# Four state-space layers on one core: B's products shared out by turn, the projection moved, seven buffers for B and C

## The chip, the cores and the metric

One core of a Trainium2 chip runs the whole program. The time is device microseconds of one execution; 18841.26 us before, the median of three runs (18840.8 to 18842.25). A smaller number is better. The engines are named as the profile names them: PE (matmul), PEld (its weight loads), DVE (vector), ACT (scalar, activation functions), POOL (GpSimd), SP (the queue that issues every DMA here).

## The reference, cut to what matters

The input is 8 images of 48 x 48 positions and 96 channels. Four residual layers follow one another, each on a group-normed input. Layers 0 and 3 are a two-dimensional selective scan, layer 1 an up- and down-sampled pointwise network, layer 2 a one-dimensional selective scan along rows and columns. The scans take nearly all the time. In one direction k of one image, with 192 inner channels d and 16 states n:

```
delta = softplus(dt_proj(x_proj(u)) + bias)             # u = silu(conv(in_proj(x)))
h[t, d, n] = exp(delta[t, d] * A[d, n]) * h[t-1, d, n] + (delta[t, d] * u[t, d]) * B[t, n]
y[t, d]    = sum_n h[t, d, n] * C[t, n]
```

There are four directions in each of these layers. In layers 0 and 3 the sum of the directions is normed, multiplied with silu(z) and projected; in layer 2 each direction is multiplied with its own silu(z) and projected.

## The kernel before

**Blocks, slots and turns.** A direction of an image is cut into 5 blocks of 10, 10, 10, 10 and 8 rows of 48 positions (480 or 384 positions). The 192 x 16 pairs (d, n) of a block are laid out as 24 units of 128 partitions. A block has 8 slots of 3 units, and 4 turns of 2 slots. The buffers `rooms` hold a turn each, and are taken in rotation. A layer has 8 x 4 x 5 = 160 blocks.

**What a turn does.** Six units pass through these steps, and every engine works through its own instructions in the order in which the program writes them (there is no scheduler):
- `make_da` (L288, ACT): exp(A * delta) into a PSUM tile for 2 units. There are two such tiles, so a pair can be made only when the scan two pairs earlier is done.
- `copy_b` (L245, ACT): the slot's B is copied to the one PSUM tile `ps_b`, from which DVE reads it. The next copy waits until DVE has read the last one.
- `make_dbu` (L264, DVE or POOL): (delta * u) * B for the slot's 3 units, a turn ahead. The table `ON_POOL` says how many of a slot's units POOL makes; POOL reads B from SBUF and needs no copy.
- `scan` (L296, DVE): the recurrence, two units at a time, three scans a turn.
- `make_hc` (L302, POOL): h * C in place, 3 units an instruction.
- `reduce` (L318, L322, L324, PE): the sums over n by matmul into `ps_y`; four slots close a sum, which ACT (layers 0 and 3, L683) or DVE (layer 2, L834) takes away in `finish`.

The loop over turns (L375 to L404) writes them in this order: scan 0, `make_hc` of the last turn's second slot, B's products of the next turn, `make_da`, `reduce` of the last turn's first slot, scan 1, `make_da`, `copy_b`, B's products, `reduce` of the second slot, `aside`, `make_hc`, `make_da` of the next turn's first pair, scan 2, `copy_b`, `finish`, `aside`.

**What goes beside it.** `aside` runs once a slot (twice a turn). In this order it issues loads of B and C (`load_bc`, L229; slots in `LOAD_BC`) and of delta and delta * u (`load_dd`, L217; slots in `LOAD_DD`) for the next block, takes one step of the generator `side`, and then runs the steps of `stage1` that fall on the slot. `stage1` prepares a block two blocks ahead. In layers 0 and 3: `s0` (slot 0) projects u to B, C and dt's input in the PSUM tile `s1`, of which there is one; `s1` (slot 1) has ACT copy it to `bcl` (L647); `s3` stores B and C to DRAM (L650) and starts dt's matmuls (L632); slots 4 and 5 add the bias (L636); `s6` (slot 6) is the Softplus (L660); slots 7 and 8 multiply with u on POOL (`make_du`, L449); slots 9 and 10 store the result to DRAM (`store_dd`, L434), whence `load_dd` broadcasts it to 128 partitions. In layer 2 the steps lie on slots 3 to 11: two convolutions (L771), a Silu in slot 6 (L778), the projection (L788), `bcl` (L793), a Softplus in slot 8 (L806), POOL's products, a Silu of z in slot 10 (L820), and the stores in slots 10 and 11.

**The side generator of layers 0 and 3** runs through an image's 160 slots: `post` of the last image (55 slots), `front` (group norm) of the next, a filler up to slot 80, and then `conv` of the next image: ten half blocks of eight steps 0 to 7, in which the matmul of z (L517) is in step 6 and the two Silus (L521, L523) in step 7. Before the change a half block starts on slot 0 of a block.

**Functions of ACT.** Exp, Softplus, Silu and Sqrt need different tables. Each change of function puts an ACT_TABLE_LOAD in ACT's queue, and another when Exp comes back.

Of the kernel before, what the change touches and what calls it, by code (L numbers as in the profile page):

```python
# [9 lines left out]
F32 = mybir.dt.float32  # L10
# [7 lines left out]
DH = 96  # L18
# [11 lines left out]
NG = 8  # L30
ORDER = [(0, sg) for sg in range(4)] + [(1, sg) for sg in range(3, -1, -1)]
LOAD_BC = (2, 3, 6, 7)
LOAD_DD = (4, 5)
NBUF = 6
UP = 96
UG = 73
UR = 7
# [1 line left out]
NM = 3  # L39
FAR = 1e30  # L40
CH = 96
ON_POOL = {1: 2, 3: 2, 5: 3, 7: 2}


DIRS_SS = [(False, False), (True, False), (False, True), (True, True)]
# [50 lines left out]
def vss_stack_kernel(ctx: ExitStack, tc: tile.TileContext, i: dict, out: bass.AP):  # L96
# [86 lines left out]
        yield  # L183


    def scans(dirs, order, restart, a, pools, ps, stage1, opening, done, side, tail):

# [46 lines left out]
        def copy_b(t):  # L234

            if t >= NG * len(blocks):
                return
            b, slot = blocks[t // NG], t % NG
            if slot == NG // 2:
                bps[t] = bps[t - 1]  # L240
                return
            if ON_POOL.get(slot) == 3:
                return
            bps[t] = ps("b", 1)
            nc.scalar.copy(bps[t][:, :bcs[t][0].shape[1]], bcs[t][0])  # L245
# [4 lines left out]
        def make_dbu(t, engine):  # L250

            if t >= NG * len(blocks):
                return
            b, slot = blocks[t // NG], t % NG
            if t // 2 not in dbus:
                dbus[t // 2] = rooms[t // 2 % (NG // 2)]
            cut = 3 - ON_POOL.get(slot, 0)
# [6 lines left out]
            engine.tensor_mul(o, du, by.unsqueeze(1).to_broadcast([P, hi - lo, by.shape[1]]))  # L264
# [13 lines left out]
        def make_da(t, pair):  # L278
            if t >= nt:
                return  # L280
            b, q = turns[t]
            da = ps("da", 2, 1024)
            das[t, pair] = da
            for u in (2 * pair, 2 * pair + 1):
                half, sg = ORDER[2 * q + u // 3]
                ci = half * 12 + sg * 3 + u % 3
                at = (u - 2 * pair) * b.m
                nc.scalar.activation(da[:, at:at + b.m], b.got[half][:, u % 3, 0, :], AF.Exp, scale=a[:, b.k, ci:ci + 1])  # L288
# [43 lines left out]
        def plan(b, at):  # L332
            b.got = {}
            sources(b, pools)
            for n, step in stage1(b).items():
                steps.setdefault(at + n, []).append(step)
# [2 lines left out]
            for step in steps.pop(t, []):  # L339
                step()  # L340

        for n, b in enumerate(blocks[:2]):
            plan(b, NG * (n - 2))
        for t in range(-2 * NG, 0):
            run(t)
        begin(0)
        begin(1)
# [27 lines left out]
        for t, (b, q) in enumerate(turns):  # L375
            at, nblk = 2 * t, t // (NG // 2)
            if q == 0:
                if nblk + 2 < len(blocks):
                    plan(blocks[nblk + 2], at)
                if b.k == order[0] and b.first:  # L380
                    beside = side(b.job)
            scan(t, 0)
            if t > 0:
                make_hc(t - 1, 1)
            make_dbu(at + 2, nc.vector)
            make_da(t, 1)
            make_dbu(at + 3, nc.gpsimd)
            if t > 0:
                reduce(t - 1, 0)
            scan(t, 1)  # L390
            make_da(t, 2)
            copy_b(at + 3)
            make_dbu(at + 3, nc.vector)
            if t > 0:
                reduce(t - 1, 1)
            aside(at)
            begin(t + 2)
            make_hc(t, 0)
# [61 lines left out]
    def ss2d(l, xin, xout, b0=0):  # L460
# [2 lines left out]

        def pool(name, bufs, **kw):
            return stack.enter_context(tc.tile_pool(name=name, bufs=bufs, **kw))
        wt, big, zp, lnp, xio = pool("wt", 1), pool("big", 3), pool("z", 1), pool("ln", 2), pool("xio", 2)
        zdr = pool("zdr", 3, space=DRAM)
        w = weights(wt, [f"{l}_{n}" for n in ("in", "cb", "xp", "dtb", "a", "d", "nw", "nb", "out")])
        dtw = wt.tile([NBC, NK, 2, DH], F32, tag="dtw", name="dtw")
# [27 lines left out]
        def load_x(b):  # L497
            nc.sync.dma_start(xpad[:C, 1:1 + H, 1:1 + W], seq(xin[b], False))

        def conv(b, blks):  # L500
            if blks[0] == BLKS[0]:
                us[b] = big.tile([DH, 2, L], F32, tag="big", name="u")
                zs[b] = zdr.tile([DH, 2, L], F32, tag="z", name="zd")
            for r0, nr in blks:
                n = nr * SEG
                for half in range(2):
                    pu = side_psum()
                    for slot in range(7):
                        for tap in ((0,), (1, 2), (3,), (4, 5), (6,), (7, 8), ())[slot]:
                            dy, dx = tap // 3, tap % 3  # L510
                            at = (2 * tap + half) * DH
                            nc.tensor.matmul(pu[:, :n], lhsT=flat[:, at:at + P],  # L512
                                             rhs=xpad[:, r0 + dy:r0 + dy + nr, dx:dx + W],
                                             start=(tap == 0), stop=(tap == 8))
                        if slot == 6:
                            pz = ps("s1", 1)
                            nc.tensor.matmul(pz[:DH, :n], lhsT=w[f"{l}_in"][:, (2 + half) * DH:(3 + half) * DH],  # L517
                                             rhs=xpad[:C, 1 + r0:1 + r0 + nr, 1:1 + W], start=True, stop=True)
                        yield
                    s = slice(r0 * W, r0 * W + n)  # L520
                    nc.scalar.activation(us[b][:, half, s], pu[:DH, :n], AF.Silu, bias=w[f"{l}_cb"][:, half:half + 1])  # L521
                    z = zp.tile([DH, BMAX], F32, tag="z", name="z")
                    nc.scalar.activation(z[:, :n], pz[:DH, :n], AF.Silu)  # L523
                    yield
                    nc.sync.dma_start(zs[b][:, half, s], z[:, :n])

# [61 lines left out]
        def side(job):  # L588
            used = 0
            more = job + 1 < nb  # L590
            if job == 0:
                for n, _ in enumerate(conv(0, BLKS[3:])):
                    if n % 2:
                        used += 1
                        yield
            if more:
                load_x(job + 1)
            if job > 0:

                for _ in range(3):  # L600
                    used += 1
                    yield
                for _ in post(job - 1):
                    used += 1
                    yield
            if more:
                for _ in front(job + 1):
                    used += 1
                    yield
                while used < 10 * NG:  # L610
                    used += 1
# [12 lines left out]

        def stage1(b):
# [33 lines left out]
                both = b.dds[:, :, 0, b.at]  # L659
                nc.scalar.activation(both, both, AF.Softplus)  # L660

            def du(half):
                return lambda: make_du(b, half, u[:, half])

            def store(half):
                return lambda: store_dd(b, half)

            return {0: s0, 1: s1, 3: s3, 4: s4, 5: lambda: biased(1), 6: s6, 7: du(0), 8: du(1),
                    NG + 1: store(0), NG + 2: store(1)}

        def so_far(b, half):
            if b.job not in yss:
# [10 lines left out]
            nc.scalar.copy(so_far(b, half), rows(y[:DH], b.n))  # L683
            return []

        dirs = DIRS_SS
# [5 lines left out]
        scans(dirs, (0, 1, 3, 2), False, a, pools, ps, stage1, opening, done, side, [])  # L692
        for _ in post(nb - 1, BLKS[:1]):
            pass
        stack.close()
# [2 lines left out]
    def lines(xin, xout):  # L698
# [56 lines left out]
        def stage1(b):  # L755
# [112 lines left out]
        load_x(0)  # L868
        for _ in front(0):
            pass  # L870
        scans(dirs, range(NK), True, a, pools, ps, stage1, opening, done, side, tail)
        stack.close()


# [286 lines left out]
```

## Time and profile before

| | |
|---|---|
| median of three runs | 18841.26 us |
| the profiled execution: time, span | 18848.6 us, 18846.8 us |
| layer 0, first to last scan | 119.3 to 5733.4 us |
| layer 1 (no scans) | to 7166.7 us |
| layer 2, first to last scan | 7166.7 to 13077.1 us |
| layer 3, first to last scan | 13204.3 to 18816.7 us |
| busy: DVE, POOL, PE, ACT | 16139.5, 15203.6, 14864.5, 13830.0 us |

The profiled execution is 1.8 us longer than its span, and 7.3 us (0.04%) longer than the median. A busy share is an average over the whole span. Layer 1 has little for DVE and POOL, so in the scan layers their shares are higher than in that average. A row of costliest groups has the line, the engine, the operation, what it writes and reads, the count, the busy time, the mean time of one, and the idle time of the engine just before such an instruction with what ended it. In a timeline, the columns are the start and the duration in microseconds; idle time before an instruction stands in brackets.

### The profile page before, as it was taken

The page shows a single profiled execution, that of the slowest core. Times are in us where ns is not written, and L with a number is a line of the kernel's source. Part 1 is how long each engine was busy: PE and PEld are TensorE (multiplying, and loading weights), DVE is VectorE, ACT ScalarE, POOL GpSimd, SP SyncE. Part 2 cuts the span into 40 slices and gives each one's busy share as a digit, 9 for nine tenths or more (in the row PEclk, how much of TensorE's full clock was granted, in tenths as well). Part 3 has the DMA queues.
Part 4 walks back from the last instruction along what each step waited for, and adds up shares of the span by engine and source line. Part 5 has one row for each costly group of instructions (what it writes and reads, how often), then busy time and mean ns, then how long its engine had stood idle before and what let it go on. Part 6 is the DMA issues. An engine that isn't in the chain of part 4 may idle for free.

```text
span 18846.8 us, 169421 instructions
## 1 busy us (share of the span) xinstructions
PE 14864.5 (79%) x53500; PEld 4298.7 (23%) x53500; DVE 16139.5 (86%) x10809; ACT 13830.0 (73%) x20502; POOL 15203.6 (81%) x8316
## 2 busy tenths in 40 slices
PE   6777777777777897888988988888677777777776
PEld 1211211211214562222222222222121121121121
DVE  7999999999993227999999999997999999999998
ACT  6777777777772227888888888886778778778776
POOL 7899899899891007888888888886899999999998
PEclk7776776776767787888888888888777777677776
DMA  4545445445453334444444444443454554554444
GB/s 138 167 166 166 167 166 168 165 166 170 161 171 60 48 46 141 154 146 153 156 147 150 151 155 148 148 154 119 164 170 162 169 170 161 169 168 161 169 166 146
DMA packets 768461, 2836.57 MB, mean 151 GB/s; under 512 B 235724, under 2 KB 298668, under 8 KB 640926
## 3 DMA queue, kind: packets, MB, share of 16 engines
q1 hardware_dynamic: 767558, 2825.75, 45.5%
q8 instruction: 418, 6.85, 0.2%
q14 instruction: 485, 3.97, 0.1%
HBM read 2377.32 MB, written 448.17 MB: 150 GB/s over the span
## 4 chain that ended last, share of the span: by engine, by line
DVE 24%; PE 21%; ACT 18%; POOL 17%; issue 12%; DMA 7%; SPq 0%; POOLq 0%; DVEq 0%; ACTq 0%
DVE dbu L296 15%; POOL dbu L302 12%; DVE dbu L264 7%; ACT ps_da L288 5%; PE ps_s L771 4%; ACT L288 4%; POOL dbu L264 4%; DMA dd<-dd 3%; PE ps_y L322 3%; DMA dd<-dds 2%; PE ps_h L1001 2%; PE ps_y L1014 2%; POOL dds L449 1%; PE ps_side L512 1%; PE ps_s L642 1%
## 5 line engine op out<-in xcount | busy, mean ns | idle before, releaser
L296 DVE TENSOR_TENSOR_SCAN dbu<-ps_da,dbu 128x968 f32<-128x968 f32 (+3 forms) x5760 | 11853.6, 2076 | 1080.1 <-ACT ps_da L288 1002.8
L302 POOL TENSOR_TENSOR dbu<-dbu,bc 128x1440 f32<-128x1440 f32 (+1 forms) x3840 | 10060.1, 2634 | 1877.1 <-DVE dbu L296 1715.4
L288 ACT ACTIVATE ps_da<-dd,w_l_a 128x484 f32<-128x484 f32 (+3 forms) x11520 | 7440.1, 650 | 2865.8 <-DVE dbu L296 2652.9
L322 PE MATMUL ps_y<-dbu,w_red 128*32 128x480 f32 (+1 forms) x23040 | 4834.2, 736 | 2581.2 <-POOL dbu L302 2578.1
L324 PE MATMUL ps_y<-dbu,w_red 128*32 128x480 f32 (+1 forms) x7680 | 4795.5, 736 | 0.0
L264 DVE TENSOR_TENSOR dbu<-dd,ps_b 128x1443 f32<-128x1443 f32 (+7 forms) x3360 | 3895.9, 1159 | 292.9 <-ACT ps_b L245 217.5
L264 POOL TENSOR_TENSOR dbu<-dd,bc 128x962 f32<-128x962 f32 (+7 forms) x1920 | 3889.3, 2026 | 96.5 <-DMA dd<-dd 50.0
L322 PEld LDWEIGHTS ps_y<-dbu,w_red 128*32 128x32 f32 x23040 | 756.2, 125 | 6399.6 <-POOL dbu L302 4693.7
L771 PE MATMUL ps_s<-xpad,w_l_cw 128*128 128x480 f32 (+1 forms) x2560 | 1753.3, 837 | 2.6 <-ACT xpad L144 1.6
L245 ACT COPY ps_b<-bc 128x482 f32<-128x482 f32 (+3 forms) x2880 | 1543.4, 536 | 283.4 <-DVE dbu L264 257.3
L512 PE MATMUL ps_side<-xpad,w_l_cw 128*128 128x480 f32 (+1 forms) x2880 | 1613.8, 688 | 5.8 <-ACT xpad L144 4.5
L288 ACT ACT_TABLE_LOAD x986 | 1265.0, 1283 | 17.3
L133 POOL MEMSET w_l_cw<- 128x1760 f32 (+1 forms) x3 | 5.8, 1942 | 1344.4 <-DVE x L981 1339.0
L642 PE MATMUL ps_s<-u,w_l_xp 96*38 96x480 f32 (+1 forms) x1280 | 932.9, 868 | 2.8 <-ACT dds L636 1.5
L632 PE MATMUL ps_s<-bcl,dtw 6*96 6x480 f32 (+1 forms) x1280 | 830.1, 735 | 125.2 <-ACT dds L636 114.9
L449 POOL TENSOR_TENSOR dds<-dds,u 96x480 f32<-96x480 f32 (+1 forms) x640 | 765.8, 1196 | 182.9 <-ACT dds L660 182.8
L318 PE MATMUL ps_y<-ysum,w_ident 96*96 96x480 f32 (+1 forms) x960 | 754.3, 875 | 134.1 <-ACT ysum L683 133.2
L512 PEld LDWEIGHTS ps_side<-xpad,w_l_cw 128*128 128x128 f32 x2880 | 571.2, 223 | 1119.3 <-issue 922.3
L771 PEld LDWEIGHTS ps_s<-xpad,w_l_cw 128*128 128x128 f32 x2560 | 517.5, 207 | 1075.5 <-issue 976.0
L324 PEld LDWEIGHTS ps_y<-dbu,w_red 128*32 128x32 f32 x7680 | 693.7, 125 | 0.0
L788 PE MATMUL ps_s<-ub,w_l_xp 96*38 96x480 f32 (+1 forms) x640 | 376.8, 724 | 271.9 <-ACT ub L778 271.8
L812 PE MATMUL ps_s<-xpad,w_l_inz 96*96 96x480 f32 (+1 forms) x640 | 506.7, 926 | 79.7 <-ACT dds L806 60.2
(147 smaller groups left out, 11761.0 us busy)
## 6 DMA issues: line engine op xcount, KB each, us to landing
dd<-dd SPq DMA_DIRECT2D x512, 1452.0 KB
bc<-bcd SPq DMA_DIRECT2D x1536, 480.0 KB
dd<-dd SPq DMA_DIRECT2D x256, 1440.0 KB
dd<-dds SPq DMA_DIRECT2D x512, 363.0 KB
dd<-dd SPq DMA_DIRECT2D x128, 1164.0 KB
bc<-bcd SPq DMA_DIRECT2D x384, 384.0 KB
dd<-dds SPq DMA_DIRECT2D x256, 360.0 KB
dd<-dd SPq DMA_DIRECT2D x64, 1152.0 KB
```

The source lines that it names most:

```text
L245: nc.scalar.copy(bps[t][:, :bcs[t][0].shape[1]], bcs[t][0])
L264: engine.tensor_mul(o, du, by.unsqueeze(1).to_broadcast([P, hi - lo, by.shape[1]]))
L288: nc.scalar.activation(da[:, at:at + b.m], b.got[half][:, u % 3, 0, :], AF.Exp, scale=a[:, b.k, ci:ci + 1])
L296: nc.vector.tensor_tensor_scan(db, da, db, 0.0, ALU.mult, ALU.add)
L302: nc.gpsimd.tensor_mul(h, h, bcs.pop(2 * t + sub)[1].unsqueeze(1).to_broadcast([P, 3, n]))
L322: nc.tensor.matmul(y[32 * g:32 * g + 32, :n], lhsT=wc["red"][:, :32], rhs=hc[:, g, b.at], start=False, stop=(slot == 3))
L324: nc.tensor.matmul(y[DH:, :n], lhsT=wc["red"][:, 32:], rhs=hc[:, 2, b.at], start=(slot == 0), stop=(slot == 3))
L449: nc.gpsimd.tensor_mul(rows(du, n), rows(dt, n), u)
L512: nc.tensor.matmul(pu[:, :n], lhsT=flat[:, at:at + P], rhs=xpad[:, r0 + dy:r0 + dy + nr, dx:dx + W], start=(tap == 0), stop=(tap == 8))
L632: nc.tensor.matmul(got["p"][:DH, :n], lhsT=dtw[2 * NS:, b.k, half, :], rhs=b.bcl[2 * NS:, :n], start=True, stop=True)
L642: nc.tensor.matmul(got["p"][:NBC, :n], lhsT=w[f"{l}_xp"][:, b.k, half, :], rhs=u[:, half], start=(half == 0), stop=(half == 1))
L771: nc.tensor.matmul(got["u", half][:, :n], lhsT=flat[:, at:at + P], rhs=shifted(off), start=(tap == 0), stop=(tap == 3))
```

## The change

- `ON_POOL` becomes two tables. In both, and before, POOL makes 9 of a block's 24 units; what differs is the slots. Before, DVE makes 4, 3, 4 and 4 units in turns 0 to 3. In layers 0 and 3 it now makes 2, 5, 2 and 6, in layer 2 it makes 4, 3, 2 and 6. POOL may now also make units of a turn's first slot, for which the loop has another call.
- `copy_b` copies no B for slots that POOL makes alone. It is 6 copies a block in layers 0 and 3 as before, and 5 in place of 6 in layer 2.
- `plan` is called a block earlier for the same slots, so that a step can lie on slot -1. In layers 0 and 3 `s0` moves to the last slot of the block before (ahead of the sums of the last turn), both `make_du` to slot 7, and the stores to slots 8 and 9.
- `LOAD_DD` goes from slots 4 and 5 to 3 and 5, in all three layers.
- There are seven buffers for B and C in place of six. `xio` goes from two buffers to one and layer 2's `zb` from three to two.
- `conv` of the next image starts five slots sooner, on slot 3 of a block. Its Silus so fall on slot 2, in the second turn. The matmul of z is put at the end of `aside`, behind the slot's steps.

```diff
-LOAD_DD = (4, 5)
-NBUF = 6
+LOAD_DD = (3, 5)
+NBUF = 7
...
-ON_POOL = {1: 2, 3: 2, 5: 3, 7: 2}
+ON_POOL_SS = {2: 1, 3: 3, 5: 1, 6: 1, 7: 3}
+ON_POOL_L2 = {3: 2, 5: 3, 6: 1, 7: 3}
...
-            if slot == NG // 2:
+            if on_pool.get(slot) == 3:
+                return
+            if slot == NG // 2 and t - 1 in bps:
                 bps[t] = bps[t - 1]
-                return
-            if ON_POOL.get(slot) == 3:
                 return
...
-        for n, b in enumerate(blocks[:2]):
+        for n, b in enumerate(blocks[:3]):
             plan(b, NG * (n - 2))
-        for t in range(-2 * NG, 0):
+        for t in range(-2 * NG - 1, 0):
             run(t)
...
-                if nblk + 2 < len(blocks):
-                    plan(blocks[nblk + 2], at)
+                if nblk + 3 < len(blocks):
+                    plan(blocks[nblk + 3], at + NG)
...
             make_dbu(at + 2, nc.vector)
             make_da(t, 1)
+            make_dbu(at + 2, nc.gpsimd)
             make_dbu(at + 3, nc.gpsimd)
...
-        wt, big, zp, lnp, xio = pool("wt", 1), pool("big", 3), pool("z", 1), pool("ln", 2), pool("xio", 2)
+        wt, big, zp, lnp, xio = pool("wt", 1), pool("big", 3), pool("z", 1), pool("ln", 2), pool("xio", 1)
...
-        def conv(b, blks):
+        def conv(b, blks, behind=lambda step: step()):
...
                         if slot == 6:
-                            pz = ps("s1", 1)
-                            nc.tensor.matmul(pz[:DH, :n], lhsT=w[f"{l}_in"][:, (2 + half) * DH:(3 + half) * DH],
-                                             rhs=xpad[:C, 1 + r0:1 + r0 + nr, 1:1 + W], start=True, stop=True)
+                            got = {}
+
+                            def gate():
+                                got["z"] = ps("s1", 1)
+                                nc.tensor.matmul(got["z"][:DH, :n], lhsT=w[f"{l}_in"][:, (2 + half) * DH:(3 + half) * DH],
+                                                 rhs=xpad[:C, 1 + r0:1 + r0 + nr, 1:1 + W], start=True, stop=True)
+                            behind(gate)
                         yield
...
-                while used < 10 * NG:
+
+                while used < 10 * NG - 5:
                     used += 1
                     yield
-                yield from conv(job + 1, BLKS)
+                yield from conv(job + 1, BLKS, tail.append)
...
-            return {0: s0, 1: s1, 3: s3, 4: s4, 5: lambda: biased(1), 6: s6, 7: du(0), 8: du(1),
-                    NG + 1: store(0), NG + 2: store(1)}
+            return {-1: s0, 1: s1, 3: s3, 4: s4, 5: lambda: biased(1), 6: s6, 7: du,
+                    NG: store(0), NG + 1: store(1)}
...
-                b.zb = up.tile([DH, 2, BMAX], F32, tag="zb", name="zb")
+                b.zb = up.tile([DH, 2, BMAX], F32, tag="zb", name="zb", bufs=2)
```

More of the change, by code (lines that the diff above doesn't have):

```diff
@@ L183, in norm_scale, with scans @@
         yield
-    def scans(dirs, order, restart, a, pools, ps, stage1, opening, done, side, tail):
+    def scans(dirs, order, restart, on_pool, a, pools, ps, stage1, opening, done, side, tail):
         blocks = [Block(job, k, blk, n == 0, n == len(BLKS) - 1, dirs[k][1])
@@ L256, in make_dbu @@
                 dbus[t // 2] = rooms[t // 2 % (NG // 2)]
-            cut = 3 - ON_POOL.get(slot, 0)
+            cut = 3 - on_pool.get(slot, 0)
             lo, hi = (0, cut) if engine is nc.vector else (cut, 3)
@@ L522, in conv @@
                     z = zp.tile([DH, BMAX], F32, tag="z", name="z")
-                    nc.scalar.activation(z[:, :n], pz[:DH, :n], AF.Silu)
+                    nc.scalar.activation(z[:, :n], got["z"][:DH, :n], AF.Silu)
                     yield
@@ L660, in s6, with du @@
                 nc.scalar.activation(both, both, AF.Softplus)
-            def du(half):
-                return lambda: make_du(b, half, u[:, half])
+            def du():
+                for half in range(2):
+                    make_du(b, half, u[:, half])
             def store(half):
                 return lambda: store_dd(b, half)
-            return {0: s0, 1: s1, 3: s3, 4: s4, 5: lambda: biased(1), 6: s6, 7: du(0), 8: du(1),
-                    NG + 1: store(0), NG + 2: store(1)}
+            return {-1: s0, 1: s1, 3: s3, 4: s4, 5: lambda: biased(1), 6: s6, 7: du,
+                    NG: store(0), NG + 1: store(1)}
         def so_far(b, half):
@@ L684, in done @@
             return []
-        dirs = DIRS_SS
+        dirs, tail = DIRS_SS, []
         load_x(0)
@@ L691, in ss2d @@
             pass
-        scans(dirs, (0, 1, 3, 2), False, a, pools, ps, stage1, opening, done, side, [])
+        scans(dirs, (0, 1, 3, 2), False, ON_POOL_SS, a, pools, ps, stage1, opening, done, side, tail)
         for _ in post(nb - 1, BLKS[:1]):
@@ L870, in lines @@
             pass
-        scans(dirs, range(NK), True, a, pools, ps, stage1, opening, done, side, tail)
+        scans(dirs, range(NK), True, ON_POOL_L2, a, pools, ps, stage1, opening, done, side, tail)
         stack.close()
```

## The prediction

> **What bounds the kernel now.** I read the busy shares first, then DVE's waits, then the timelines of DVE and ACT over one turn.
>
> ```profile
> PE 14864.5 (79%) x53500; PEld 4298.7 (23%) x53500; DVE 16139.5 (86%) x10809; ACT 13830.0 (73%) x20502; POOL 15203.6 (81%) x8316
> ```
> ```profile
> DVE dbu L296 <- ACT ps_da L288: 1002.8, 826, 4.1
> ...
> ACT bcl L647 <- PE ps_s L642: 340.4, 136, 5.8
> ```
>
> DVE is the fullest engine, and layer 1 leaves it half idle. From 470 to 5180 us (layer 0) it is busy 93%, POOL 91%, ACT 78%, PE 76%. So a scan layer is DVE's work plus DVE's idle time, and the idle time is what can be won. Summed over the timeline between first and last scan it is 394 us in layer 0, 389 in layer 3, 529 in layer 2. Most of it is one wait: the scan stands ready, and ACT has not made its exp. The two timelines show why. First a Softplus (layer 0, end of turn 3):
>
> ```profile
> 3730.47 1.63 DVE L264 TENSOR_TENSOR dbu<-dd,ps_b 128x1443 f32<-128x1443 f32 x1
> 3732.02 2.16 DVE L296 TENSOR_TENSOR_SCAN dbu<-ps_da,dbu 128x968 f32<-128x968 f32 x1
> 3734.10 0.63 DVE L264 TENSOR_TENSOR dbu<-dd,ps_b 128x481 f32<-128x481 f32 x1
> ...
> 3737.57 2.17 DVE L296 TENSOR_TENSOR_SCAN dbu<-ps_da,dbu 128x968 f32<-128x968 f32 x1 [0.69 <-ACT ps_da L288]
> ```
> ```profile
> 3732.14 0.57 ACT L245 COPY ps_b<-bc 128x482 f32<-128x482 f32 x1 [0.18 <-DVE dbu L264]
> 3732.72 1.28 ACT L660 ACT_TABLE_LOAD   x1
> 3734.01 0.85 ACT L660 ACTIVATE dds<-dds 96x768 f32<-96x768 f32 x1
> 3734.88 1.28 ACT L288 ACT_TABLE_LOAD   x1
> 3736.17 1.37 ACT L288 ACTIVATE ps_da<-dd,w_l_a 128x484 f32<-128x484 f32 x2
> ```
>
> The exp of the next turn's first pair stands behind the Softplus and two loads: it ends 7.07 us after the turn's first product began. DVE would be there after 6.4. Then a Silu of `conv`, a slot later:
>
> ```profile
> 2011.15 1.28 ACT L521 ACT_TABLE_LOAD   x1
> 2012.44 0.66 ACT L521 ACTIVATE u<-ps_side,w_l_cb 96x480 f32<-96x480 f32 x1
> 2013.00 0.56 ACT L523 ACTIVATE z<-ps_s 96x480 f32<-96x480 f32 x1
> 2013.58 1.28 ACT L288 ACT_TABLE_LOAD   x1
> ```
> ```profile
> 2016.27 2.17 DVE L296 TENSOR_TENSOR_SCAN dbu<-ps_da,dbu 128x968 f32<-128x968 f32 x1 [1.87 <-ACT ps_da L288]
> ```
>
> By turn, layer 0's idle time is: 113 us ahead of the first scan of turn 0 (Softplus), 134 ahead of its second (Silu, some 70 blocks at 1.87), 53 ahead of turn 1's second scan, 38 put down to POOL, the rest small waits for PE. Layer 3 repeats this. The 53 belong to the second wait above: ACT's copy to `bcl` stands for PE's projection, which PE runs only after sums that wait for POOL. Layer 2 has 238 ahead of turn 0 (Silu of slot 6), 112 ahead of turn 1 (Softplus), 20 ahead of turn 2, 63 at its adds (L849, L851), 59 for `dd` loads, 37 others.
>
> **What the Trainium skill says.** "ScalarE: Activation LUTs", section "What ACT_TABLE_LOAD costs", gives 1283 ns for a load and some 1380 ns of drain. The trace agrees on the load; it shows the next instruction 0.02 us later, so I use 1.28. "Perfetto Trace Analysis", section "Identifying Performance Opportunities", says that a repeated bubble can mean that too few buffers are there; here it is the order of ACT's queue. "GPSIMD Engine Reference", section "Specifications", says that POOL shares its SBUF interface with DVE and contends when DVE has two SBUF inputs. DVE's scans and products read one of theirs from PSUM, and POOL's `make_hc` stays at 2.73 to 2.75 us; so I keep POOL's durations when DVE becomes denser.
>
> **The change, step by step** (10-row blocks; starts of successive DVE instructions: scan 2.09, product of three units 1.55, of one 0.54, of two by halving the difference 1.05).
>
> 1. *Units by turn, layers 0 and 3.* DVE's 15 units a block stay: four products of three and three of one (7.8 us) become three of three and three of two (7.8). Work: no gain. Turn 3 gets longer: from its first product, 1.55 + 2.09 + 1.55 + 2.09 = 7.3 us to the next turn, against ACT's 7.1 to 7.3 (8-row or 10-row Softplus). The Softplus wait goes, but for 8-row blocks (two in ten at about 1 us). 113 becomes 25: **88 us**.
> 2. *Silus in the second turn.* The 134 go. In turn 1 DVE takes 1.55 + 2.09 + 1.05 + 2.09 = 6.8 us after its first scan; ACT takes a copy that ends at 2.2, the Silus 3.8, the exp 1.37: 7.4. New wait 0.6 us in 70 blocks, more in the short ones: 45. **90 us**. z's matmul now stands on PE behind `bcl`'s copy, which ends about 8.5 us into the block; the Silus need it at 11.
> 3. *Projection a slot sooner.* It (2 to 2.8 us on PE) runs before the sums of turn 3, and `bcl` finds it done: **50 of the 53 us**. The price: those sums end later, perhaps 6.7 us into the block; ACT asks at 7.2. Its cover is this half microsecond, plus 2 us until a late ACT stops DVE.
> 4. *POOL.* Per block 8 `make_hc` at 2.69, 21.5; units: three of one and two of three. A product of one unit has no row; by the step from 1.89 (two) to 2.74 (three) it is 1.04, at least 0.9, so 8.6 against 8.4; `make_du` 2.0 to 2.5 and 0.3 of memsets. 32.4 to 32.9, against DVE's 32.9 plus side work. Turns 0 and 2 hold 9.2 us of POOL against 7.3 of DVE, turns 1 and 3 give it back; POOL runs up to 2.5 us late. Its units for turn 1 end at 8.3 us, DVE wants them at 10.9. I take 0.25 us of new waits a block, from 0 to 1: **minus 80** over 320 blocks. PE's sums and side matmuls come later with POOL: **minus 20** a layer.
> 5. *Stores and loads, layers 0 and 3.* On SP both `dd` stores go out a slot sooner, `dd`'s first load too; the store of z moves from slot 0 to 3, between that load and B's and C's store. SP will wait there for the Silus until about 14 us into the block; the loads behind it are needed after 25. One `xio` buffer makes 64 loads of x wait on SP for the store before them, a few us each. All hidden by loads that land several us early: 0.
> 6. *Layer 2.* Its turn 0 is as before, so the Softplus's 112 stay. Turn 3 gains a us of DVE work from turn 2, against the 1.5 us mean wait behind the Silu of slot 6. But the Silu also needs a convolution (7.7 us on PE). Where rows are convolved (half of the blocks) PE is done 6 us earlier: 1.0 us won, 80 us. Where columns are, it ends just as ACT comes (the second half's Silu waits up to 0.8 us), and the wait only changes its name: 0.2 us, 16. **96 us**, from 0 to 180. One copy of B fewer (0.55 us of ACT) lies beside other work. `dd`'s first load now goes out ahead of the second store. The first store took 10.2 us to land with the other beside it and should take less; its 59 us of waits are held by the shorter turns before it: 0, from -60 to 50. The second load and B's and C's behind it come 1 to 2 us later, with about 2 us to spare. `zb` with two buffers: DVE's last read is a turn before ACT's write: 0.
>
> Sum: 2 x (88 + 90 + 50 - 20) - 80 + 96 = 432 us. From the profiled execution's 18848.6 that gives 18417; less the 7 us by which it lies over the median, **18410**.
>
> **The rivals.**
> - *POOL becomes the bound* in layers 0 and 3. For: 91% busy already, and 32.9 us a block is DVE's own work. Against: POOL waits for DVE's scans for 391 us in 4600. Blocks would take some 34.5 us in place of 35.1 (both lengths mixed). 320 x 0.6 = 190 and half of layer 2: 18600. Chance 0.15.
> - *Everything hides*: no new wait after the Silus or from POOL, layer 2 wins 180, and the small PE waits go too. 432 + 80 + 90 + 40 + 84 = 726: 18115. Chance 0.08.
> - *The sums come too late* (slower). Projection and side matmuls now stand ahead of turn 3's sums on PE, and POOL's `make_hc` ahead of these is later. ACT takes the finished sum in its own order; if it is done later than 9 us into the block, each further us goes to the exp of turn 1 and so to DVE. It decides against the change from 11.3 us on. At 12.5 us the cost is 3 us in 320 blocks less the sum above: 18840 + 960 - 430 = 19370. For: `bcl` waited as much as 5.8 us for PE. Against: PE has 24% free here. Chance 0.06.
> - *Layer 2's chain and the exchange of waits return all*: within 0.2% of before. Chance 0.03.
>
> **The numbers.** Forecast 0.68, the others as given. Within 0.2%, about 38 us, a measurement of this kernel cannot tell a change from none. Faster: 0.68 + 0.15 + 0.08 = 0.91. Same 0.03, slower 0.06. The range 18150 to 18730 holds the forecast's own bounds (the unknowns of 4, 2 and 6 together make some 200 us either way) and most of the first two rivals.
>
> **What would show it.** Right: DVE's waits for ACT's exp (L288) fall from 1003 us to under 500; no wait ahead of turn 0's second scan; about 0.6 us ahead of turn 2's first scan in blocks with Silus; `bcl`'s 340 us gone; POOL above 93% in layers 0 and 3; layer 2's wait ahead of turn 0 shorter in row blocks alone. Wrong: DVE waiting for POOL's products, ACT waiting for `ps_y`, or a layer 0 longer than 5500 us.

## The result, and the profile after

The changed kernel takes **18727.88 us** (median of four runs, 18719.84 to 18741.66); the kernel before takes 18841.75 us beside it. The ratio is 0.994, 95% interval 0.9922 to 0.9957: 114 us faster, where 432 were forecast. The profiled execution has a span of 18720.7 us, 126 less than before. The scan layers, from first to last scan in the timelines of the two kernels, show where that comes from:

| us | before | after | change | forecast |
|---|---|---|---|---|
| layer 0 | 5614.1 | 5481.3 | -133 | -168 |
| layer 2 | 5910.4 | 6055.0 | **+145** | -96 |
| layer 3 | 5612.4 | 5483.1 | -129 | -168 |

(The forecast's 168 are 88 + 90 + 50 - 20 and half of the 80 for POOL.) Three quarters of the gain in layers 0 and 3 came. Layer 2 turned against the change.

The busy shares of the profile after:

```profile
PE 14799.0 (79%) x53500; PEld 4319.5 (23%) x53500; DVE 16219.3 (87%) x10329; ACT 13661.6 (73%) x20342; POOL 15238.6 (81%) x8639
```

DVE has fewer instructions than before and 80 us more work. In a stretch of layer 0, from 500 to 5000 us, it is now busy for 4330 us (96%; before 4180), POOL for 4206 (93%; before 4083).

DVE's waits after the change (engine and line, what it waited for, us in total, times, longest):

```profile
DVE dbu L298 <- ACT ps_da L290: 511.7, 579, 3.4
...
DVE dbu L266 <- ACT ps_b L247: 353.1, 94, 88.4
```

The second of these rows was there before, but with six waits only:

```profile
DVE dbu L264 <- ACT ps_b L245: 217.5, 6, 88.0
```

and this is the row of ACT's waits, after the change, to which it leads:

```profile
ACT ps_b L247 <- DMA bc<-bcd: 345.4, 141, 12.4
```

The wait for the exp has halved (1002.8 before), and `bcl`'s 340.4 us for the projection are down to 6.2. In their place stands a chain that the scan layers did not have before: DVE's product waits for ACT's copy of B, and the copy waits for the DMA that brings B. Between the first and the last scan of layer 2 these are 136 us of DVE and 322 us of ACT. The 217 us of before, which are still there, all lie outside the scan layers as the table counts them, at their starts.

The steps aimed at layers 0 and 3 can be seen in one stretch of layer 0. DVE after, then ACT after, in columns of start, duration, instruction and idle time in brackets:

```profile
2059.07 1.64 DVE L266 TENSOR_TENSOR dbu<-dd,ps_b 128x1443 f32<-128x1443 f32 x1
2060.61 4.26 DVE L298 TENSOR_TENSOR_SCAN dbu<-ps_da,dbu 128x968 f32<-128x968 f32 x2
...
2079.42 2.17 DVE L298 TENSOR_TENSOR_SCAN dbu<-ps_da,dbu 128x968 f32<-128x968 f32 x1 [0.53 <-ACT ps_da L290]
```
```profile
2057.68 1.28 ACT L668 ACT_TABLE_LOAD   x1
2058.98 1.00 ACT L668 ACTIVATE dds<-dds 96x960 f32<-96x960 f32 x1
2060.00 1.28 ACT L290 ACT_TABLE_LOAD   x1
2061.30 1.37 ACT L290 ACTIVATE ps_da<-dd,w_l_a 128x484 f32<-128x484 f32 x2
```

The Softplus at 2057.68 stands beside a turn with two products of three units; the exp is done at 2062.67, just as turn 0's first scan follows turn 3's last without a gap (the pair of scans from 2060.61). The Silus, in turn 1 (ACT from 2074.30, the exp behind them done at 2079.39), cost turn 2's first scan 0.53 us here, where the prediction had 0.6.

Layer 2 is another picture. SP issues the stores of `dd` (delta and delta * u), its loads and the loads of B and C in one queue. The timeline of SP before, one block of layer 2 (issue time, time in issue):

```profile
9025.08 0.73 SPq L434 DMA_DIRECT2D dd<-dds  x1
9025.85 0.54 SPq L229 DMA_DIRECT2D bc<-bcd  x1
9026.83 1.21 SPq L434 DMA_DIRECT2D dd<-dds  x1
9035.37 6.36 SPq L217 DMA_DIRECT2D dd<-dd  x2
9042.26 3.21 SPq L229 DMA_DIRECT2D bc<-bcd  x2
```

and after:

```profile
9008.11 0.74 SPq L437 DMA_DIRECT2D dd<-dds  x1
9008.90 0.54 SPq L231 DMA_DIRECT2D bc<-bcd  x1
9019.06 0.51 SPq L219 DMA_DIRECT2D dd<-dd  x1
9019.67 0.73 SPq L437 DMA_DIRECT2D dd<-dds  x1
9031.00 0.53 SPq L219 DMA_DIRECT2D dd<-dd  x1
9031.58 1.24 SPq L231 DMA_DIRECT2D bc<-bcd  x2
```

Before, both stores (360 KB each) were in flight together: the first landed 10.2 us after its issue, the second 14.3, and the B and C of the last row were issued 17.2 us after the first store. After, `dd`'s first load stands between the stores, and SP waits at it until the first store has landed (10.9 us). Only then does the second go out (11.2 us). The B and C of the last row are issued 23.5 us after the first store, 6.3 us later than before. ACT and DVE pay for it in the timelines of the same block after:

```profile
9038.50 0.56 ACT L247 COPY ps_b<-bc 128x480 f32<-128x480 f32 x1 [4.71 <-DMA bc<-bcd]
```
```profile
9039.10 1.66 DVE L266 TENSOR_TENSOR dbu<-dd,ps_b 128x1440 f32<-128x1440 f32 x1 [3.12 <-ACT ps_b L247]
```

### The profile page after: what moved, and what is told of

The parts are those of the page before. It is cut to its first block, busy times and chain, and to the rows that moved or that the text cites. A ratio compares the mean times of both kernels' runs of the same rounds, so it can differ in the third digit from the quotient of the medians.

```text
span 18720.7 us, 168607 instructions
## 1 busy us (share of the span) xinstructions
PE 14799.0 (79%) x53500; PEld 4319.5 (23%) x53500; DVE 16219.3 (87%) x10329; ACT 13661.6 (73%) x20342; POOL 15238.6 (81%) x8639
## 4 chain that ended last, share of the span: by engine, by line
POOL 29%; DVE 16%; DMA 16%; PE 15%; issue 14%; ACT 9%; SPq 1%; POOLq 0%; DVEq 0%; ACTq 0%
POOL dbu L304 20%; DVE dbu L298 10%; DMA dd<-dds 8%; POOL dbu L266 6%; DMA bc<-bcd 6%; DVE dbu L266 4%; ACT ps_da L290 4%; PE ps_y L324 2%; POOL dds L452 2%; PE ps_h L1010 2%; PE ps_s L780 2%; PE ps_y L1023 2%; ACT L290 1%; PE ps_side L515 1%; PE ps_a L1000 1%
## 5 line engine op out<-in xcount | busy, mean ns | idle before, releaser
L266 DVE TENSOR_TENSOR dbu<-dd,ps_b 128x962 f32<-128x962 f32 (+5 forms) x2880 | 3831.1, 1330 | 387.8 <-ACT ps_b L247 353.1
L266 POOL TENSOR_TENSOR dbu<-dd,bc 128x481 f32<-128x481 f32 (+5 forms) x2240 | 3911.1, 1761 | 245.4 <-DMA bc<-bcd 136.7
L247 ACT COPY ps_b<-bc 128x482 f32<-128x482 f32 (+3 forms) x2720 | 1450.8, 533 | 463.4 <-DMA bc<-bcd 345.4
L515 PE MATMUL ps_side<-xpad,w_l_cw 128*128 128x480 f32 (+1 forms) x2880 | 1575.3, 676 | 17.7 <-ACT u L528 12.7
L640 PE MATMUL ps_s<-bcl,dtw 6*96 6x480 f32 (+1 forms) x1280 | 867.0, 765 | 65.1 <-ACT dds L644 57.7
L650 PE MATMUL ps_s<-u,w_l_xp 96*38 96x480 f32 (+1 forms) x1280 | 843.4, 790 | 20.9 <-ACT z L530 17.9
L808 PE MATMUL ps_s<-bcl,dtw 6*96 6x480 f32 (+1 forms) x640 | 459.1, 859 | 500.1 <-ACT bcl L802 500.1
```

The source lines that it names most:

```text
L515: nc.tensor.matmul(pu[:, :n], lhsT=flat[:, at:at + P], rhs=xpad[:, r0 + dy:r0 + dy + nr, dx:dx + W], start=(tap == 0), stop=(tap == 8))
L640: nc.tensor.matmul(got["p"][:DH, :n], lhsT=dtw[2 * NS:, b.k, half, :], rhs=b.bcl[2 * NS:, :n], start=True, stop=True)
L650: nc.tensor.matmul(got["p"][:NBC, :n], lhsT=w[f"{l}_xp"][:, b.k, half, :], rhs=u[:, half], start=(half == 0), stop=(half == 1))
```

## The experiments

Times are medians; ratios are to the kernel before on the same chip, with 95% intervals. "After" is the changed kernel's 18727.88.

### Layer 2: the loads or the units?

**Layer 2's loads back on slots 4 and 5**, all else as after:

```diff
+LOAD_DD_L2 = (4, 5)
-                if slot in LOAD_DD:
-                    load_dd(blocks[nblk], LOAD_DD.index(slot))
+                at_dd = LOAD_DD_L2 if restart else LOAD_DD
+                if slot in at_dd:
+                    load_dd(blocks[nblk], at_dd.index(slot))
```

> The changed kernel, with layer 2's dd loads in slots 4 and 5 again; layers 0 and 3 keep 3 and 5. Theory A, the order of the loads: in layer 2 the first dd load, put ahead of the second store, makes SP wait twice in a row for a store to land (about 11 us each), so that B and C of the second slot pair come 6 us later and ACT's copy of B waits for them. With the loads back, ACT's 310 us of waits for B go to under 30 us, layer 2 falls from 6055 us to 5800-5870, and the whole to 18480-18550. Theory B, the units: layer 2's new table of units is at fault; then layer 2 stays above 6000 us and the whole within 40 us of 18728.

Measured: 18530.71 us, ratio 0.9831 [0.9817, 0.9846], 197 us under after. Layer 2 takes 5869.0 us, 186 less. ACT's waits of `ps_b` for B fall from 345 to 22 us, none of them in layer 2, and in DVE's waits the old `dd` wait is back, twice as large as before the change (59 us in layer 2):

```profile
DVE dbu L267 <- DMA dd<-dd: 116.7, 100, 4.2
```

Against the kernel before, layer 2 is then 41 us shorter.

**Layer 2's units back**, loads as in the change:

```diff
-ON_POOL_L2 = {3: 2, 5: 3, 6: 1, 7: 3}
+ON_POOL_L2 = {1: 2, 3: 2, 5: 3, 7: 2}
```

> The changed kernel, with layer 2's units of B shared out as before the change (and so six copies of B a block); the dd loads stay in slots 3 and 5. Theory A (order of the loads): B still comes late in layer 2, ACT still waits some 300 us for it, layer 2 stays above 6000 us, the whole is 18700-18800. Theory B (the units): layer 2 falls back to about 5910 us, the whole to about 18580.

Measured: 18741.36 us, ratio 0.9943 [0.9928, 0.9957], layer 2 at 6069.8 us. ACT's waits for B stay at 242 us, 221 of them in layer 2. The units are not the cause.

**The kernel before with nothing but layer 2's loads moved** (`LOAD_DD_L2 = (3, 5)` by the same edit as in the first experiment):

> The kernel before, with one thing of the change: layer 2's dd loads in slots 3 and 5. Theory A (order of the loads): layer 2 gets longer by 100-250 us, from 5910 to 6010-6160, and the whole is 18940-19090. Theory B (the units): within 40 us of 18842.

Measured: 19001.74 us, ratio 1.0081 [1.0066, 1.0096]: 155 us slower. Layer 2 is 6081.4 us, and the chain stands in ACT's waits of this kernel as it does after the change:

```profile
ACT ps_b L246 <- DMA bc<-bcd: 250.7, 126, 12.0
```

One number of the change, the first slot of `LOAD_DD` in layer 2, costs 171 us there when it is the only edit and 186 among the others.

**The store, made faster.** Why does a store of 360 KB take 11 us? Its target has an outermost dimension of 3. The Trainium skill, "DMA: Bandwidth & Descriptors", section "Why a DMA increments its semaphore by 16 and not by 1", says that a transfer runs on the largest number of engines up to 16 that divides the outermost sizes of both sides: three here, and sixteen if 32 rows are outermost. The trace agrees: the semaphore (the counter that tells of the landing) of the store issued at 9008.11 makes three late steps, at 9015.83, 9016.25 and 9018.99. The load of B issued beside it has thirteen of its sixteen steps by 9012.41 and the last three only from 9017.01 to 9020.16. So the same bytes as three stores of 32 partitions:

```diff
-        nc.sync.dma_start(b.dd[half].rearrange("j (g m) -> g j m", g=3), b.dds[:, half].rearrange("p t m -> p (t m)"))
+        for g in range(3):
+            nc.sync.dma_start(b.dd[half][:, 2 * b.m * g:2 * b.m * (g + 1)],
+                              b.dds[32 * g:32 * g + 32, half].rearrange("p t m -> p (t m)"))
```

> The changed kernel, with each dd store issued as three stores of 32 partitions in place of one of 3 x 32 (six issues a block more on SP). Theory F: a dd store takes 11 us to land because three DMA engines carry its 96 rows; as three stores of 32 rows it runs on all sixteen and lands in 3-5 us. Then B no longer comes late in layer 2 although the loads stand in slots 3 and 5: ACT's 310 us of waits for B fall below 40, layer 2 goes from 6055 to 5750-5860 us, and the whole to 18400-18530. Rival: the landing is bound by the latency of writes or by the other transfers; then a store still takes over 8 us and the whole stays within 60 us of 18728.

Measured: 18390.91 us, ratio 0.976 [0.9743, 0.9776], 337 us under after and more than was expected. Layer 2 falls to 5751.7 us, 303 less; layer 0 stays (5482.7), since its stores go out three slots and more ahead of the loads. In its table of DMA issues (KB each, median us from issue to landing) the stores of layer 2's 10-row blocks are

```profile
dd<-dds SPq DMA_DIRECT2D x768, 120.0 KB, 2.7
```

and SP's timeline shows what is left of the wait, with the order of the change:

```profile
9026.88 1.24 SPq L438 DMA_DIRECT2D dd<-dds  x3
9028.46 0.52 SPq L231 DMA_DIRECT2D bc<-bcd  x1
9029.91 0.51 SPq L219 DMA_DIRECT2D dd<-dd  x1
```

The three land by 9029.8, 2.9 us after the first issue, each with sixteen steps of its semaphore within 0.4 us; the load goes out at once. The second store's three parts stand behind that load of 1440 KB and land 9.3 us after their first issue, but B and C then go out 13.6 us after the first store, for 17.2 before the change and 23.5 after it. ACT's waits for B fall to 14 us, none of them in layer 2. Whether the kernel before would win as much by this edit was not run.

### Layers 0 and 3: each part undone

**The units by turn undone** (`ON_POOL_SS` set to the old table):

```diff
-ON_POOL_SS = {2: 1, 3: 3, 5: 1, 6: 1, 7: 3}
+ON_POOL_SS = {1: 2, 3: 2, 5: 3, 7: 2}
```

> The changed kernel, with the units of B of layers 0 and 3 shared out as before; layer 2 and all else as changed. Theory D, the units cover ACT's table loads: turns 1 and 3 lose 1 us of DVE work each, so that DVE's idle time ahead of turn 0 (Softplus) goes from 38 back to about 110 us a layer and the one ahead of turn 2 (Silus) from 52 to about 120; the whole rises by 200-300 us to 18930-19030. Rival: the gain of layers 0 and 3 came from the moved Silus and projection, and where the units lie matters little; then the whole stays within 60 us of 18728.

Measured: 18860.27 us, ratio 1.0009 [1.0, 1.0017]: 132 us over after. The wait ahead of turn 0's first scan in layer 0 goes from 38.5 us back to 106.7, as expected; what turn 2's first scan waits for ACT goes from 27 to only 45. So the theory holds for the Softplus, at half of the forecast whole. Part of the difference is that the group norm on DVE gets 18 us a layer cheaper by this edit (below).

**The Silus back in the first turn:**

```diff
-                while used < 10 * NG - 5:
+                while used < 10 * NG:
```

> The changed kernel, with the next image's conv starting on slot 0 of a block again, so that its Silus fall on slot 7. Theory D: the Silus stand again between the exps of turn 0's first and second scan, which now follow each other 1 us sooner, so that DVE waits 2.5 us ahead of the second scan in some 70 blocks, 175 us a layer, while the 40 us ahead of turn 2 go; the whole rises by 200-280 us to 18930-19010. Rival: the Silus only change the place of the wait; then within 60 us of 18728.

Measured: 18889.57 us, ratio 1.0025 [1.0017, 1.0032]: 162 us over after. Turn 0's second scan waits 169 us in layer 0, and turn 2's wait is gone: the theory holds, with a smaller whole than expected.

**The projection back in slot 0:**

```diff
-            return {-1: s0, 1: s1, 3: s3, 4: s4, 5: lambda: biased(1), 6: s6, 7: du,
+            return {0: s0, 1: s1, 3: s3, 4: s4, 5: lambda: biased(1), 6: s6, 7: du,
```

> The changed kernel, with the projection of layers 0 and 3 in slot 0 again, behind the sums of the last turn. Theory E: ACT's copy to bcl waits for PE again (340 us in both layers) and DVE behind it ahead of turn 1's second scan, 50 us a layer and more since POOL and the sums run later than before the change; the whole rises by 80-200 us to 18810-18930. Rival: the projection ahead of the sums delays these and the side matmuls that DVE waits for (60 us a layer now, 30 before); then nothing or a gain of up to 60 us, 18670-18740.

Measured: 19264.36 us, ratio 1.0223 [1.0207, 1.0238]: 536 us over after, several times what was expected. In ACT's waits of this kernel:

```profile
ACT bcl L655 <- PE ps_s L650: 914.2, 315, 6.2
```

Before the change this wait was 340.4 us in 136 cases; now it comes in nearly every one of 320 blocks. POOL and PE of this kernel show why:

```profile
2059.82 0.86 POOL L452 TENSOR_TENSOR dds<-dds,u 96x384 f32<-96x384 f32 x1
2060.64 2.73 POOL L304 TENSOR_TENSOR dbu<-dbu,bc 128x1440 f32<-128x1440 f32 x1
```
```profile
2063.42 1.02 PE L324 MATMUL ps_y<-dbu,w_red 128*32 128x480 f32 x3 [3.64 <-POOL dbu L304]
...
2067.61 1.80 PE L650 MATMUL ps_s<-u,w_l_xp 96*38 96x480 f32 x4
```

The first row is the second of two `make_du` (the first began at 2058.67). Both now stand ahead of the turn's last `make_hc`, so PE's last sums wait 3.64 us for POOL, and the projection, behind these sums and a convolution, ends at 2069.41. ACT reaches the `bcl` copy 1.94 us before that. Behind the copy stand the exp of turn 1, z's matmul and the Silus, so the delay is paid twice: in layer 0, 249 us ahead of turn 1's second scan and 112 in turn 2. In the kernel after, PE's timeline has the projection from 2061.13 to 2062.93 and the 3.27 us wait for POOL behind it, from 2063.9: it runs in time in which PE would wait anyway.

**Where DVE's extra work is.** In layer 0 the group norm's four one-column instructions with two inputs in SBUF cost 22.7 us before and 66.3 after, with the same count. One case, DVE and then POOL in the kernel after:

```profile
2473.27 5.93 DVE L183 SCALAR_TENSOR_TENSOR shift<-gm,rs 96x1 f32<-96x1 f32 x1
```
```profile
2473.73 5.42 POOL L304 TENSOR_TENSOR dbu<-dbu,bc 128x1440 f32<-128x1440 f32 x2
```

An instruction on one column ends only when two POOL products back to back are over. It has two inputs in SBUF. Six of the seven in layer 0 look like this one (5.91 to 5.93 us): each begins in the last half microsecond of a POOL product, and a short copy and two products follow without a gap. The Trainium skill, "Trainium Architecture — The Big Picture", section "What this means for kernel authors", says of the port pair that DVE and POOL share that it is "an exclusive lock (not a bandwidth split)". The test: give those instructions one input in PSUM, where a spare column of the norm's own tile is free (`apart` is set in layers 0 and 3; elsewhere the old lines stay).

```diff
-        nc.vector.tensor_sub(dev, mv[:, 0:1], gm)
-        nc.vector.tensor_mul(dev, dev, dev)
-        nc.vector.tensor_add(dev, dev, mv[:, 1:2])
+        if apart:
+            d = got["p"][:C, 1:2]
+            nc.vector.tensor_sub(d, mv[:, 0:1], got["p"][:C, :1])
+            nc.vector.tensor_sub(dev, mv[:, 0:1], got["p"][:C, :1])
+            nc.vector.tensor_mul(d, dev, d)
+            nc.vector.tensor_add(dev, d, mv[:, 1:2])
...
-        nc.vector.reciprocal(rs, rs)
...
-        nc.vector.scalar_tensor_tensor(shift, gm, -1.0, rs, ALU.mult, ALU.mult)
+        if apart:
+            nc.vector.reciprocal(got["p"][:C, 1:2], rs)
+            nc.vector.reciprocal(rs, rs)
+            nc.vector.scalar_tensor_tensor(shift, gm, -1.0, got["p"][:C, 1:2], ALU.mult, ALU.mult)
```

> The changed kernel; in layers 0 and 3 the group norm's one-column products on DVE read one of their two operands from PSUM in place of SBUF (one more subtraction and one more reciprocal). Theory C, the shared interface: these one-column instructions took up to 5.3 us each because both operands come from SBUF and POOL, now rarely idle, has the interface; then they fall to below 0.4 us each, about 8 us an image, 50-60 us a layer, and the whole falls by 80-120 us to 18610-18650. Rival: they are long for another reason (a wait that the trace does not show, such as for the operand written just before), then they stay long and the whole stays within 30 us of 18728.

Measured: 18607.39 us, ratio 0.987 [0.9854, 0.9887], 120 us under after: 56 in layer 0, 64 in layer 3. The same instruction in this kernel's DVE timeline, begun, like the one above, while POOL was in the middle of a product (2443.70 to 2446.44):

```profile
2446.16 0.13 DVE L192 SCALAR_TENSOR_TENSOR shift<-gm,ps_side 96x1 f32<-96x1 f32 x1
```

All seven in layer 0 take 0.13 us. Here the trace agrees with the skill: the instruction with two inputs in SBUF is held for whole POOL instructions, and not slowed in part. It also puts a price on the lock: up to two POOL products, 5.9 us, for 0.13 us of work.

What changed is where these instructions fall in POOL's order, more than how busy POOL is (91% before, 93% after). In the kernel with the old units they cost 48.8 us in layer 0: three of the four are back at their times of before, and the last, the one shown above, still takes 29.3 us for 3.3 before. The new units so account for some 18 us of the 43; which other part moved the last one was not tried.

**Six buffers for B and C** (`NBUF = 6`, all else as after):

> The changed kernel with six buffers for B and C. Theory A: in layer 2 the load of B that comes late stands behind the second dd load on SP and not behind a buffer, and in layers 0 and 3 the loads land many us early; so the whole stays within 60 us of 18728. Rival: POOL now runs later and gives buffers back later, so that with six of them loads wait for POOL and B comes late in all three layers; then the whole rises by 100-300 us to 18830-19030.

Measured: 18723.15 us, ratio 0.9935 [0.992, 0.995]; all layers within 5 us of after. The seventh buffer moves nothing here.

### Put together

**Spread store and norm in PSUM**, the two edits above on the kernel after:

> The changed kernel with both mends: dd stores as three of 32 partitions, and the norm's one-column products of layers 0 and 3 with one operand in PSUM. The causes lie in different layers (337 us, nearly all in layer 2, and 120 us in layers 0 and 3), so both gains should add: 18240-18310. Rival: they meet in DVE's queue and add only in part: above 18330.

Measured: **18269.22 us, ratio 0.9694 [0.9679, 0.9708]**. It is 459 us under after; alone the two edits won 337 and 120, so the gains add, as expected. This beats both kernels.

**The same with layer 2's loads on slots 4 and 5:**

> As e10_spread_norm, with layer 2's dd loads in slots 4 and 5. Theories A and F: with stores that land in 2-3 us the order of load and store no longer matters, so it is within 40 us of e10_spread_norm. Rival: the order itself matters (dd's first load is a slot sooner in e10): 60-150 us slower than e10_spread_norm.

Measured: 18276.46 us, ratio 0.9699 [0.9682, 0.9715]. That is 7 us over the version with 3 and 5, within the spread of the runs: with the spread stores, the order of loads no longer matters.

**Spread store and norm, with the two `make_du` apart on slots 7 and 8 and the stores a slot later:**

```diff
-            def du():
-                for half in range(2):
-                    make_du(b, half, u[:, half])
+            def du(half):
+                return lambda: make_du(b, half, u[:, half])
...
-            return {-1: s0, 1: s1, 3: s3, 4: s4, 5: lambda: biased(1), 6: s6, 7: du,
-                    NG: store(0), NG + 1: store(1)}
+            return {-1: s0, 1: s1, 3: s3, 4: s4, 5: lambda: biased(1), 6: s6, 7: du(0), 8: du(1),
+                    NG + 1: store(0), NG + 2: store(1)}
```

> As e10_spread_norm, with POOL's two products of a block in slots 7 and 8 of layers 0 and 3 and the stores in 9 and 10, as before the change. Theory E: both products in slot 7 hold back POOL's last product with C of a block, and with it the sums, by 1 us; apart they give DVE's waits for PE and ACT back in part: 20-80 us faster than e10_spread_norm. Rival: the projection ahead of the sums already covers this, or the second product then holds back units of B: within 20 us or slower.

Measured: 18262.74 us, ratio 0.969 [0.9676, 0.9705], 6 us under the version with both in slot 7, which the intervals do not tell apart; the rival holds. In layer 0 the last sums end 1.1 us sooner than with both products in slot 7 (median 4.3 us after the block's first scan, for 5.4), and nothing is won. With the projection ahead of them, late sums of this size do not hurt.

## Why the prediction was wrong in size

The sign was right: faster, and by the mechanisms of steps 1 to 3. The size was not: 114 us for 432. That the measured time still lies in the stated range, by 2 us, is luck: layer 2 alone missed by more than the 200 us that the range allowed for the unknowns of steps 2, 4 and 6 together. Of the 315 us that the three layers together lack, 241 are layer 2's and 74 those of layers 0 and 3.

1. *Units by turn.* Layer 0's wait ahead of turn 0's first scan goes from 113 to 38.5 us; 25 were forecast. Right, 75 for 88. Undone among the other parts, it costs 132 us in all, and layer 0's idle time rises by 75.
2. *Silus in the second turn.* Of the 134 us, 4.6 are left. Turn 2's first scan now waits 52 us (27 put down to ACT, 13 to POOL, 12 to issue), for 45. Right, 77 for 90 net; undone, 162 us in all.
3. *The projection.* Turn 1's second scan waits 3 us for 53. The term was right in the change as a whole. Undone alone it costs 536 us, five times the 100 that the prediction gave it: with both `make_du` in slot 7 and POOL denser, the sums are late in nearly every block, and only the projection's place ahead of them keeps that from DVE. Behind them it ends 10.5 us after the block's first scan (median in layer 0), for 8.9 before the change. This is the old wait of `bcl`, grown, and not the rival of late sums: ACT's copy of the finished sum starts 7.1 us into the block, after the change and in this kernel too. Which of POOL's two additions makes the sums late with the projection behind them was not tried apart.
4. *POOL.* Most of the 80 us did not come: idle time put down to POOL in layer 0 is 45 us, before 38 (13 of the 45 are those of turn 2's first scan, counted under 2 as well). Layer 3 too has 7 more. A product of one unit takes 1.035 us, by the estimate 1.04. DVE's small waits for PE rose by some 30 us a layer, for 20, and turn 3's second scan has a new wait of 22 for ACT. POOL did not become the bound, though its rival's 18600 is as near to the measured time as the rival of no change.
5. *Stores, loads and buffers in layers 0 and 3.* Nothing, as said: DVE waits 5 us for DMAs in layer 0, for 9 before, and six buffers do as well. The single `xio` buffer was not undone.
6. *Layer 2, the step that failed.* The prediction let `dd`'s first load pass the second store and wrote that the first store "took 10.2 us to land with the other beside it and should take less". Without the other it takes 10.9. So the two stores, which had overlapped, came one after the other, and B was not "1 to 2 us later, with about 2 us to spare" but 6.3 us. The step priced what stands behind the load at 1 to 2 us and left out the second store: SP stops at a load that waits, so the second store goes out 11.6 us after the first (1.8 before) and then takes its own 11.2, for which the second load waits. Layer 2's idle time rose from 529 to 652 us. The expected part is there, the wait ahead of turn 0 fell from 238 to 118, and the 59 for `dd` loads are gone; against it stand 136 of DVE for the copy of B, 46 more ahead of turn 1 and 122 more of `gated` (L843) for PE, whose matmuls behind `bcl` wait because the copy to `bcl` stands behind the copy of B on ACT (PE's waits for that copy went from 170.5 to 500.1 us).

   With the loads put back, the other parts win 41 us in layer 2 for the forecast's 96. The wait ahead of turn 0 is then 86 us, so 152 are won there and not 96, and the split by direction was wrong: blocks of rows win 74 us and blocks of columns 78, where 80 and 16 were forecast. What takes it back are the waits for `dd` loads, 59 us before and 115 now, and those of `gated` for PE, 28 and 78. The prediction had the first at 0, from -60 to 50, and did not have the second; why it rose was not taken apart.

A **missing term** made the difference in layers 0 and 3: DVE's own work. The prediction named the shared SBUF interface and dismissed it, since DVE's scans and products read PSUM. It did not look for DVE instructions that don't. The norm's do, and they now fall where POOL's products follow each other without a gap: 43 us a layer more than before. With idle time at 233 us in layer 0 (394 before), 161 less, the two make 118 of the 133 us won; the other 15 are small differences in DVE's other instructions, not assigned. That the idle time fell nearly as the terms add up, 161 us of 168, is in part luck: items 1 and 2 won 26 us less than forecast, turn 3's second scan and PE cost some 33 more, and the 33 that POOL did not cost made good much of it. One reading was off and bore no weight: layer 1 leaves DVE not half idle but busy for a fifth (284 of 1410 us before the change).

Of the signs named beforehand: DVE's wait for the exp is 512 us (500 was the mark), 0.53 us stand ahead of turn 2 in the case shown, `bcl`'s wait is gone, POOL is at 93%, and layer 0 is under 5500. Layer 2's wait ahead of turn 0 became shorter in column blocks as well, which the prediction had excluded. ACT's waits for `ps_y` with its copy of the finished sum (L692), named as a sign of the prediction being wrong, went from 22.5 to 59.5 us in the whole run, which is little. None of the signs looked at layer 2's queue, where it failed.

## What to carry to other kernels

Before a waiting load is moved ahead of a store in one queue, list everything behind it and ask whether the stores still overlap; a store that takes 10 us in company need not be faster alone, so look first at how its outermost dimension cuts it. A stall that a change removes may be what hides another: undo parts singly before calling any of them small. And when the work of a co-working engine becomes denser or changes its order, look for the smallest instructions that share a resource with it, not only at the largest.

## What the runs showed of the hardware that was not expected

- A store of 96 partitions written with an outermost size of 3 (360 KB) landed 10.9 to 11.2 us after its issue. The same bytes as three stores of 32 partitions landed within 2.9 us, and in 9.3 us behind a load of 1440 KB. This edit alone is worth 337 us in the changed kernel, three times the change.
- A DVE instruction on 96 x 1 elements with both inputs in SBUF took 5.93 us while POOL ran two products without a gap, and 0.13 us with one input in PSUM, begun at the same point of POOL's order.
